# Two transformer layers on one core: the opening of layer 0, with its Q and K traffic spread over three queues and side work moved later

## The chip, the core and the metric

The kernel runs on one core of a Trainium2 chip. A core has five engines, each with its own instruction queue that it works through in order: TensorE (PE in the profile, its weight loads PEld), VectorE (DVE), ScalarE (ACT), GpSimd (POOL) and SyncE (SP), which here only issues DMA transfers. ScalarE and GpSimd can issue DMA transfers too, from the same in-order queue as their arithmetic. Engines wait for each other by semaphores. Sixteen DMA engines carry all transfers of the core.

The metric is the time of one execution in microseconds on the device. Lower is better.

## The reference

Two layers work on x of 2 x 1024 x 256. Each adds an attention and a feed-forward part to x, both computed from the same layernorm of x. Only layer 0 is touched by the change:

```python
xn = layernorm(x)
# attention: 32 query heads and 8 key/value heads of 8 columns, causal
q = rope((xn @ Wq + bq).heads(32));  k = rope((xn @ Wk + bk).heads(8));  v = (xn @ Wv + bv).heads(8)
scores = where(kpos > qpos, -inf, q @ repeat(k, 4).T / sqrt(8))
attn = softmax(scores) @ repeat(v, 4) @ Wo + bo
# feed-forward in e4m3: every operand of a product is rounded to e4m3 first
ffn = (gelu(xn8 @ w_gating8[0]) * (xn8 @ w_gating8[1]))8 @ w_linear8
x = x + attn + ffn
```

Layer 1 is an attention with 16 heads over 512-token sequences and a gated feed-forward part with ternary weights.

## The kernel before

**Tiles.** The 2048 tokens are 16 tiles of 128 (`xs`), four to a chunk; a batch `b` has two chunks `c` and eight tiles `i`. `layernorm` (L153) is a generator: statistics of four tiles to a step, then the inverse root (`rsqrt`, L139: VectorE, a square root on ScalarE with its own activation table, VectorE), then per chunk four normalised rows `xn`, and a step of eight transposes `lnt` on TensorE and two copies into `xnT` on ScalarE.

**Q and K.** Q and K are split into three bf16 parts each, and a score is a sum of products of parts over 64 + 35 rows. `project` (L713) multiplies `xnT` with the weights into two PSUM banks, applies bias and rope with two `scalar_tensor_tensor` on VectorE (L729) and adds them; `split` (L701) makes the three parts by turns of ScalarE casts (L704, L707) and subtractions (L706, L708), on VectorE for batch 0's chunk 0, on GpSimd otherwise. The parts are rearranged by a round trip through DRAM: written to a scratch (`kscr`, `qscr`) and loaded back in the order that the score products need. For K, `prepare_k` (L736) writes once and loads 18 pieces of 8 rows x 4 x 512. For Q, `prepare_q` (L756) makes one half `e` of the heads for a whole chunk and writes each of its four tiles by itself; `load_q` (L766) loads one tile: for each half two pieces of 24 rows, one of 16 and one of 8, each row 4 KB. `qlast` are four buffers for the last 35 rows, cleared at the start.

**Softmax.** The maximum of every row is needed before the exponentials. `max_unit` (L835) multiplies queries with keys for a few heads and VectorE reduces the product (L858); `take_max` splits a tile's maxima into three parts, and `turn_max` (L879) transposes them on TensorE, copies them to `mt` on ScalarE, writes them to DRAM (`mscr`) and loads them into three rows of `qlast`. Only then can `weigh` (L905, one unit of head group `u` and key tile `j`) multiply again, now with the maximum subtracted, and ScalarE takes the exponential (L920). `gather` accumulates p times v.

**The order.** TensorE's order in layer 0 is written by hand: a loop over slots (`one_slot`, L1108), one to a unit of weighing. In each slot the maxima of later tiles are advanced by a credit so that they run ahead of the weighing, one piece of the feed-forward work is emitted (`pieces`, `pieces_left`), and delayed steps fall due (`after`). When the maxima reach tile number n of the order, the list `extra[n]` is set free, one entry with each following unit. In `extra` stand, for tile 0, chunk 1's layernorm and its K; for tile 1, chunk 1's Q and V; for tile 2, the layernorm of batch 1 (`second`); for 4, 6 and 7, batch 1's Q, K and V. The other engines are ordered by a scheduler that takes instructions as they become ready. `tc.issue_after(ins)` holds a block's instructions behind `ins` on that instruction's own engine; `behind()` does so with `mark`, the last normalised row or the last subtraction of a split on VectorE.

**The feed-forward weights.** `weights0` (L203) loads six pieces of 512 KB and rounds each to e4m3 in five steps on VectorE (`e4m3`, L182: L190, L193, L195, L198, L200). Before Q and K are prepared, the first load is issued from SP and three steps of the first conversion are set on VectorE, behind `mark`.

**The start.** SP issues, in this order: four tiles of x, rope of chunk 0, the three weights, five small constants, four more tiles of x, the first feed-forward piece; then K's write and 18 loads, Q's eight writes and the loads of tiles 0 to 3, rope of chunk 1 and `wo` among them, and the other tiles of x.

## Time and profile before

| | |
|---|---|
| median of three runs | 1212.17 us (1210.58 to 1214.08) |
| the profiled execution's own time | 1211.61 us |
| its span, first to last instruction | 1209.9 us |
| PE busy | 1026.2 us, 85%, 7228 matmuls |
| DVE busy | 741.5 us, 61%, 1416 instructions |
| ACT busy | 571.7 us, 47% |
| POOL busy | 348.4 us, 29% |
| mean granted TensorE clock | 0.897 |
| first reduction of a maximum (L858) | 48.21 us |
| first complete weighing (L910) | 104.47 us |

The span is the time from the first to the last instruction of the profiled execution; the own time of that execution is 1.7 us more. Lines of the timeline give start and duration in microseconds, the engine, the source line, the operation with the tile that it writes and those that it reads, how many were merged, and in brackets how long the engine had been idle and what ended that. SPq is SP's queue of DMA issues: its durations are those of issuing, not of the transfer. Lines of waits give the waiting instruction, what it waited for, the total, how often, and the longest. Lines of windows give the stretch, its length, busy time of PE, PEld, DVE, ACT and POOL with instruction counts, the granted TensorE clock as a share of full speed, the mean busy share of the 16 DMA engines, and GB/s. Layer 0 takes up about the first 800 us.

### The profile page before, as it was taken

How to read it: one execution, taken by the hardware profiler on the slowest of the kernel's cores; microseconds unless marked ns; L12 is line 12 of the kernel's file. 1: busy time of each engine (PE TensorE's matmuls, PEld its weight loads, DVE VectorE, ACT ScalarE, POOL GpSimd, SP SyncE). 2: the span in 40 equal slices, each digit the busy share in tenths (PEclk: the TensorE clock that was granted, in tenths of full speed). 3: DMA queues.
4: the chain of work that ended last, by engine and by line, in shares of the span. 5: the costliest groups of instructions: out<-in, count | busy, mean ns of one | idle time of the engine just before them, and what ended most of it. 6: DMA issues, size and time to landing. Idle time of an engine off the chain costs nothing.

```text
span 1209.9 us, 18918 instructions
## 1 busy us (share of the span) xinstructions
PE 1026.2 (85%) x7228; PEld 490.2 (41%) x7228; DVE 741.5 (61%) x1416; ACT 571.7 (47%) x990; POOL 348.4 (29%) x400
## 2 busy tenths in 40 slices
PE   5464888896888989897989998988999999998884
PEld 2232332232232222232323333344676676675673
DVE  6677988995877998789895889162223323322220
ACT  1113353661645757576766776731414414424421
POOL 2023233314144021612125337553313213212100
PEclk8676796996898989898999999998999999998885
DMA  6631001103001010101010110047211421411202
GB/s 194 158 91 37 22 15 38 27 2 90 1 20 33 2 26 18 35 1 24 4 27 2 25 27 5 3 49 114 41 28 46 75 41 45 80 36 29 45 11 53
DMA packets 79011, 48.99 MB, mean 40 GB/s; under 512 B 31720, under 2 KB 73704, under 8 KB 78920
## 3 DMA queue, kind: packets, MB, share of 16 engines
q1 hardware_dynamic: 75960, 43.58, 16.9%
q0 software_dynamic: 2960, 4.20, 1.6%
q8 instruction: 57, 0.93, 0.3%
q14 instruction: 34, 0.28, 0.1%
HBM read 33.59 MB, written 15.73 MB: 41 GB/s over the span
## 4 chain that ended last, share of the span: by engine, by line
PE 55%; DVE 26%; ACT 5%; issue 4%; POOL 4%; DMA 4%; SPq 1%; ACTq 0%; POOLq 0%; DVEq 0%
DVE mx L858 14%; PE f1gu L609 9%; PE acc L940 8%; PE s L910 7%; PE f1o L640 5%; PE m L846 4%; PE sk L519 3%; PE sq L484 3%; PE gu L283 3%; ACT p L527 2%; PE m L823 2%; PE acc L534 1%; PE ao L585 1%; PE pqk L435 1%; ACT p L920 1%
## 5 line engine op out<-in xcount | busy, mean ns | idle before, releaser
L858 DVE TENSOR_REDUCE mx<-m 128x1 f32<-128x512 f32 (+3 forms) x608 | 373.1, 654 | 101.5 <-PE m L846 63.1
L920 ACT ACTIVATE p<-s 128x512 f32<-128x512 f32 x576 | 307.1, 604 | 146.3 <-PE s L910 144.8
L940 PE MATMUL acc<-p,v 128*9 128x512 f32 x1152 | 173.7, 626 | 0.6 <-ACT o L949 0.2
L846 PE MATMUL m<-k,qmain 64*128 64x512 bf16 (+3 forms) x384 | 96.6, 376 | 49.2 <-DVE mx L858 33.0
L924 POOL TENSOR_SCALAR_AFFINE_SELECT p<-p 128x512 f32<-128x512 f32 x128 | 84.6, 685 | 170.1 <-ACT p L920 169.9
L609 PE MATMUL f1gu<-xnT,wgu 128*128 128x512 f32 x256 | 118.5, 607 | 0.0
L846 PE MATMUL m<-kmain,qmain 64*128 64x512 bf16 (+3 forms) x384 | 82.8, 336 | 22.9 <-DVE mx L858 20.7
L846 PEld LDWEIGHTS <-qmain 64*128 64x128 bf16 x768 | 50.4, 101 | 88.4 <-issue 62.9
L621 POOL TENSOR_TENSOR sq<-h 128x512 f32<-128x512 f32 x28 | 29.2, 1041 | 190.1 <-DVE h L617 190.1
L617 DVE TENSOR_TENSOR h<-f1gu,h 128x512 f32<-128x512 f32 x32 | 22.1, 692 | 99.7 <-PE f1gu L609 96.4
L910 PE MATMUL s<-qlast,k 35*128 35x512 bf16 x288 | 66.5, 411 | 14.6 <-DMA qlast<-mscr 14.6
L910 PE MATMUL s<-qmain,k 64*128 64x512 bf16 x288 | 68.6, 412 | 11.8 <-ACT ob L251 6.2
L823 PEld LDWEIGHTS <-ident_h 64*128 64x128 bf16 x832 | 44.9, 97 | 82.5 <-issue 60.3
L823 PE MATMUL m<-mask_q,ident_h 64*128 64x128 bf16 (+3 forms) x832 | 75.3, 222 | 2.5 <-DVE mx L858 2.2
L910 PE MATMUL s<-qmain,kmain 64*128 64x512 bf16 x288 | 64.0, 391 | 6.0 <-ACT p L920 3.2
L910 PEld LDWEIGHTS <-k 64*128 64x128 bf16 (+1 forms) x576 | 21.2, 97 | 115.7 <-issue 108.2
L609 PEld LDWEIGHTS f1gu<-xnT,wgu 128*128 128x128 f32 x256 | 48.0, 197 | 49.2 <-issue 49.1
L492 DVE TENSOR_REDUCE m<-sq 128x16 f32<-128x2048 f32 x16 | 36.7, 2292 | 45.3 <-PE sq L484 43.8
L910 PE MATMUL s<-qlast,klast 35*128 35x512 bf16 x288 | 61.3, 387 | 0.0
L640 PE MATMUL f1o<-k,h 128*128 128x256 f32 x256 | 60.4, 393 | 0.0
L640 PEld LDWEIGHTS f1o<-k,h 128*128 128x128 f32 x256 | 50.1, 197 | 8.7 <-issue 1.1
L983 POOL TENSOR_TENSOR x<-x,aos 128x256 f32<-128x256 f32 x16 | 13.1, 817 | 140.1 <-ACT aos L982 140.0
(265 smaller groups left out, 1572.4 us busy)
## 6 DMA issues: line engine op xcount, KB each, us to landing
qmain<-qscr SPq DMA_DIRECT2D x64, 96.0 KB
qkv<-all SPq DMA_DIRECT2D x16, 384.0 KB
qscr<-ptq SPq DMA_DIRECT2D x32, 96.0 KB
x<-in_x SPq DMA_DIRECT2D x16, 128.0 KB
qmain<-qscr SPq DMA_DIRECT2D x32, 64.0 KB
qs<-qkv SPq DMA_DIRECT2D x16, 128.0 KB
ks<-qkv SPq DMA_DIRECT2D x16, 128.0 KB
vs<-qkv SPq DMA_DIRECT2D x16, 128.0 KB
```

Of the source, the lines that this page charges most:

```text
L283: nc.tensor.matmul(ps, wg[:, u, k, hc * P : (hc + 1) * P], xq[:, k, :], start=(k == 0), stop=(k == 1))
L484: nc.tensor.matmul(ps[:, s, r, :], columns(q, slice(S * s, S * s + HD + 8), 4 * b + r), columns(k, slice(S * s, S * s + HD + 8), 4 * b + r ...
L492: nc.vector.tensor_reduce(m, ps, AX.X, ALU.max, negate=True)
L609: nc.tensor.matmul(ps[g], wgu[:, k, g * HID + hc * P : g * HID + (hc + 1) * P], xnT[n][:, k, :], start=(k == 0), stop=(k == 1),)
L640: nc.tensor.matmul(po, hs[hc // 2][:, hc % 2, i * P : (i + 1) * P], wp[:, hc, :], start=(hc == 0), stop=(hc == NHC - 1),)
L823: nc.tensor.matmul(out[e][:, :, lo:], ident_h[rows, t, :], rhs.to_broadcast([HALF, out[e].shape[1], P - lo]), start=start and t == 0, stop ...
L846: nc.tensor.matmul(sc[e][:, s * width : (s + 1) * width], qst[b, i][0][rows, p, :], kst[b][0][rows, p // 4, lo : lo + width], start=not fo ...
L858: reduced = nc.vector.tensor_reduce(mx[b, i][:, part, e, pairs[0] : pairs[0] + n], sc[e][:, : n * width].rearrange("p (s k) -> p s k", s=n ...
L910: nc.tensor.matmul(sc[e], kst[b][n][rows, u, j * P : (j + 1) * P], qst[b, i][n][rows, 4 * u : 4 * u + 4, :], start=n == 0, stop=n == 1,)
L920: nc.scalar.activation(p, sc[e], AF.Exp, scale=scale)
L924: nc.gpsimd.affine_select(out=by_head, in_=by_head, compare_op=ALU.is_ge, fill=0.0, base=0, pattern=[[0, 4], [1, P]], channel_multiplier=-1,)
L940: nc.tensor.matmul(acc[32 * s : 32 * s + HD0 + 1, :], vst[b][:, j, 4 * G + s, :], ps[s], start=(j == 0), stop=(j == i),)
```

## The change

The change rearranges the opening of layer 0. What is computed stays the same.

- Four of the small constants are issued first of all, from ScalarE's queue; `bo` from SP after the second four tiles of x.
- The feed-forward weights' first load is issued from GpSimd like the others. `next(conversions)`, which only issues that load, stands after K's preparation, and the three conversion steps before it are gone: they become pieces of the slot loop (`pieces_left` 156 + 18 instead of 156 + 15).
- K's write is issued from GpSimd except for batch 0's chunk 0, and there three of the 18 loads go to GpSimd.
- Q's four writes per half become one of 12 pieces of 128 columns, from GpSimd, or from ScalarE for batch 0's chunk 0. The scratch keeps the four tiles of a chunk together, so a tile's load now reads blocks of 8 rows that lie apart; tile 0's loads are issued from ScalarE.
- Chunk 1's Q, K and V move from the start of the maxima of tiles 0 and 1 to those of tile 2, K after Q; the layernorm of batch 1 from tile 2 to tile 3, with its VectorE instructions held behind the last reduction.
- `mt` has two buffers.

```diff
@@ -106,11 +106,10 @@
         nc.sync.dma_start(out=rope[:, :, c * 512 : (c + 1) * 512], in_=a["rope0"][:, :, c * 512 : (c + 1) * 512])
 
     def load_small():
-        nc.sync.dma_start(out=bq, in_=a["bq"])
-        nc.sync.dma_start(out=bk, in_=a["bk"])
-        nc.sync.dma_start(out=inv_freq, in_=a["inv_freq"][None, :].to_broadcast([P, 8]))
-        nc.sync.dma_start(out=bv_bc, in_=a["bv"][None, :].to_broadcast([P, 64]))
-        nc.sync.dma_start(out=bo_bc, in_=a["bo"][None, :].to_broadcast([P, D]))
+        nc.scalar.dma_start(out=bk, in_=a["bk"])
+        nc.scalar.dma_start(out=bq, in_=a["bq"])
+        nc.scalar.dma_start(out=bv_bc, in_=a["bv"][None, :].to_broadcast([P, 64]))
+        nc.scalar.dma_start(out=inv_freq, in_=a["inv_freq"][None, :].to_broadcast([P, 8]))
 
     def load_weights(pool, names):
         w = []
@@ -211,8 +210,7 @@
         def load(n):
             st = stage[n % 4]
             if n < 4:
-
-                (nc.sync if n < 1 else nc.gpsimd).dma_start(out=st, in_=a["w_gating"][n // 2, n % 2 * P : n % 2 * P + P, :])
+                nc.gpsimd.dma_start(out=st, in_=a["w_gating"][n // 2, n % 2 * P : n % 2 * P + P, :])
             else:
                 nc.gpsimd.dma_start(
                     out=st.rearrange("p (c d) -> p c d", d=D),
@@ -744,24 +742,25 @@
                     engine.memset(kst[b][1].bitcast(F32), TWO_ONES)
                 parts = project(wk, 0, P, bk, b, c, f"k{b}{c}")
                 scr = dram.tile([3, HD0, 16, 512], BF, tag="kscr", name=f"kscr{b}{c}")
-                nc.sync.dma_start(out=scr.rearrange("a d n t -> (d n) a t"), in_=parts)
+                (nc.gpsimd if b or c else nc.sync).dma_start(out=scr.rearrange("a d n t -> (d n) a t"), in_=parts)
                 for e in range(2):
                     for n, (_, ka) in enumerate(MAIN + [LAST]):
                         lo = HALF * e + HD0 * (n % 8)
-                        nc.sync.dma_start(
+
+                        queue = nc.sync if b or c or e == 0 or n % 3 else nc.gpsimd
+                        queue.dma_start(
                             out=kst[b][n // 8][lo : lo + HD0, :, c * 512 : (c + 1) * 512],
                             in_=scr[ka, :, 4 * e : 4 * e + 4, :],
                         )
 
             def prepare_q(b, c, e):
                 parts = project(wq, e * P, 2 * P, bq[:, :, e], b, c, f"q{b}{c}{e}")
-                for i in range(4):
-                    scr = scratch[b, 4 * c + i, e] = dram.tile(
-                        [3, P, P], BF, tag=f"qscr{i}{e}", name=f"qscr{b}{4 * c + i}{e}"
-                    )
-                    nc.sync.dma_start(
-                        out=scr.rearrange("a p t -> p a t"), in_=parts[:, :, i * P : (i + 1) * P]
-                    )
+                scr = scratch[b, c, e] = dram.tile([3, 4, P, P], BF, tag=f"qscr{e}", name=f"qscr{b}{c}{e}")
+
+                (nc.gpsimd if b or c else nc.scalar).dma_start(
+                    out=scr.rearrange("a i p t -> p (a i) t"),
+                    in_=parts.rearrange("p a (i t) -> p (a i) t", i=4),
+                )
 
             def load_q(b, i):
 
@@ -770,12 +769,12 @@
                     qlast[len(qst) % len(qlast)],
                 ]
                 for e in range(2):
-                    parts = scratch[b, i, e].rearrange("a (d h) t -> (a d) h t", d=HD0)
-                    for n, lo, rows in ((0, 0, 24), (0, 24, 24), (0, 48, 16), (1, 0, 8)):
-                        start = 16 if n else 0
-                        last_load[0] = nc.sync.dma_start(
-                            out=qst[b, i][n][HALF * e + lo : HALF * e + lo + rows],
-                            in_=parts[start : start + rows],
+                    parts = scratch[b, i // 4, e][:, i % 4].rearrange("a (d h) t -> a d (h t)", d=HD0)
+                    for n, row, lo, hi in ((0, 0, 0, 3), (0, 24, 0, 3), (0, 48, 0, 2), (1, 0, 2, 3)):
+                        row += HALF * e
+                        last_load[0] = (nc.sync if b or i else nc.scalar).dma_start(
+                            out=qst[b, i][n][row : row + HD0 * (hi - lo)].rearrange("p h t -> p (h t)"),
+                            in_=parts[lo:hi],
                         )
 
             def prepare_v(b, c):
@@ -879,7 +878,7 @@
             def turn_max(b, i, parts):
                 ps = ps_t.tile([P, P], BF, tag="t", name=f"mt{b}{i}")
                 nc.tensor.transpose(ps[: 3 * NH0], parts.rearrange("p a h -> p (a h)"), ident_bf)
-                mt = pool.tile([3 * NH0, P], BF, tag="mt", name=f"mts{b}{i}", bufs=1)
+                mt = pool.tile([3 * NH0, P], BF, tag="mt", name=f"mts{b}{i}", bufs=2)
                 nc.scalar.copy(mt, ps[: 3 * NH0])
                 scr = dram.tile([3 * NH0, P], BF, tag="mscr", name=f"mscr{b}{i}")
                 nc.sync.dma_start(out=scr, in_=mt)
@@ -996,13 +995,12 @@
             spare = [x.rearrange("p u t -> p (u t)").bitcast(F32) for x in spare]
             conversions = weights0(pool, [x[:, n * 1024 : (n + 1) * 1024] for x in spare for n in range(2)])
             rest_of(layernorm(0, [0], pool, ps_t, "t"))
-            weights = next(conversions)
             with behind():
                 for t in qlast:
                     nc.vector.memset(t, 0.0)
-                for _ in range(3):
-                    next(conversions)
             prepare_k(0, 0)
+            with behind():
+                weights = next(conversions)
             for e in range(2):
                 prepare_q(0, 0, e)
             load_q(0, 0)
@@ -1033,14 +1031,18 @@
                 with behind():
                     next(first)
 
+            def next_second():
+                with tc.issue_after(reduced.ins):
+                    next(second, None)
+
             def pause():
                 pass
 
             extra = {
-                0: [lambda: next(first)] + [next_first] * 2 + [lambda: next(first), lambda: prepare_k(0, 1)],
-                1: [lambda e=e: prepare_q(0, 1, e) for e in range(2)] + [lambda: prepare_v(0, 1)],
-                2: [lambda: next(second)] * 4 + [pause] * 2 + [lambda: next(second), lambda: next(second)]
-                + [pause, lambda: rest_of(second)],
+                0: [lambda: next(first)] + [next_first] * 2 + [lambda: next(first)],
+                2: [lambda e=e: prepare_q(0, 1, e) for e in range(2)]
+                + [lambda: prepare_k(0, 1), lambda: prepare_v(0, 1)],
+                3: [next_second] * 4 + [pause] * 2 + [next_second] * 2 + [pause] + [next_second] * 2,
                 4: [lambda e=e: prepare_q(1, 1, e) for e in range(2)],
                 6: [lambda: rest_of(conversions)]
                 + [lambda c=c: prepare_k(1, c) for c in range(2)]
@@ -1087,7 +1089,7 @@
             credit = share = 0.0
             cost_left = sum(cost for _, cost, _ in maxima)
             pairs_left = sum(4 * (i + 1) for _, i in order)
-            pieces_left = 156 + 15
+            pieces_left = 156 + 18
             done_at = {}
 
             def advance():
@@ -1147,10 +1149,11 @@
                 next_late()
 
 
+    load_small()
     load_rope(0)
     w0 = load_weights(zp, ("wk0", "wq0", "wv0"))
-    load_small()
     load_x(4, 8)
+    nc.sync.dma_start(out=bo_bc, in_=a["bo"][None, :].to_broadcast([P, D]))
     qlast = [zp.tile([P, NH0 // 2, P], BF, tag=f"qlast{n}", name=f"qlast{n}") for n in range(4)]
     tables = []
     attention0(w0, qlast, tables)
```

## The prediction

> **What bounds the kernel now.** I read the shares of busy time first, then the times of the opening from the timeline, then who waited for whom between 60 and 110 us, and last the busy time by stage. The whole run has TensorE busy for 85% of its span and VectorE for 61%. That average hides the place of this change, so the first two lines below are TensorE and VectorE in 40 slices of 30 us.
>
> ```profile
> PE   5464888896888989897989998988999999998884
> DVE  6677988995877998789895889162223323322220
> ...
> 20.52 0.69 DVE L190 TENSOR_SCALAR few<-spare_main 128x1024 int32<-128x1024 int32 x1 [6.79 <-DMA spare_main<-in_w_gating]
> 21.13 0.75 DVE L729 SCALAR_TENSOR_TENSOR k00y<-k00p,bk,rope 128x512 f32<-128x512 f32 x1
> 28.23 0.38 SPq L747 DMA_DIRECT2D kscr<-ptk  x1
> 30.78 6.53 SPq L751 DMA_DIRECT2D k<-kscr  x18
> 36.70 0.69 DVE L708 TENSOR_TENSOR ptq<-restq,ptq 128x512 bf16<-128x512 f32 x1 [0.68 <-ACT ptq L707]
> 37.40 4.29 SPq L762 DMA_DIRECT2D qscr<-ptq  x8
> 41.74 1.28 SPq L776 DMA_DIRECT2D qmain<-qscr  x3
> 47.66 0.58 PE L846 MATMUL m<-k,qmain 64*128 64x128 bf16 x7 [1.62 <-DMA qlast<-qscr]
> 48.21 1.29 DVE L858 TENSOR_REDUCE mx<-m 128x4 f32<-128x512 f32 x2 [6.13 <-PE m L846]
> ```
>
> TensorE is at half or less for 120 us. VectorE sits for 6.79 us before L190, an FFN weight conversion whose data has not come, and K's first step (L729), ready since 16.4 us, stands behind it. Only after the splits come 18 K loads, 8 Q writes and the Q loads, all one after another on SP. The first maximum is taken at 48.21 us. The next stage has its own wait:
>
> ```profile
> POOL restq L706 <- ACT ptq L704: 20.9, 2, 20.1
> ACT rs_sln L145 <- DVE rs_vln L144: 17.4, 1, 17.4
> ...
> PE s L910 <- DMA qlast<-mscr: 14.6, 1, 14.6
> ```
>
> ScalarE waits 17.4 us with the square root of the second layernorm at the head of its queue. Behind it stands chunk 1's Q split, behind that GpSimd's, behind that SP's write of Q, and behind that the maxima of tile 0; so TensorE's first weighing (L910) waits 14.6 us, until 104.47. The last view is busy time by stage:
>
> ```profile
> core 0: us, PE busy (x) PEld busy (x) DVE busy (x) ACT busy (x) POOL busy (x), PEclk, DMA share, GB/s
> 0.00:48.20 48.20, 20.83 (x61) 10.39 (x62) 31.11 (x89) 8.06 (x13) 8.20 (x25) 0.79 0.60 171
> 48.20:106.60 58.40, 32.59 (x209) 18.15 (x208) 39.59 (x84) 9.05 (x15) 12.46 (x12) 0.65 0.36 96
> 106.60:151.50 44.90, 36.46 (x268) 16.44 (x267) 42.18 (x76) 17.95 (x35) 13.49 (x17) 0.77 0.12 28
> 151.50:166.00 14.50, 13.28 (x112) 5.36 (x110) 11.14 (x18) 11.02 (x22) 2.45 (x4) 1.00 0.01 1
> ...
> 291.50:297.50 6.00, 4.93 (x18) 2.46 (x18) 3.94 (x11) 0.00 (x0) 0.16 (x1) 0.50 0.33 94
> 142.00:145.00 3.00, 1.32 (x9) 0.59 (x10) 3.00 (x5) 0.00 (x0) 1.38 (x1) 0.86 0.72 172
> ```
>
> Before 106.6 us (the second unit of weighing, u1) VectorE is idle for 17.1 + 18.8 us: latency rules. From there to 151.5 it is busy for 42.2 of 44.9 us: VectorE rules. Then TensorE does, with 13.3 of 14.5. So what is gained in the first stage must still pass one in which VectorE has no room.
>
> **The change, part by part.** Durations are of this execution, whose own time is 1211.61 us; the median of three is 1212.17.
>
> *Conversion moved off the first split; small loads to ScalarE's queue.* K's first L729 can start when the four memsets of qlast end (13.7 us), the second when its matmuls end (16.4), so it ends at 17.2 instead of 23.1. The rest of K's split took 5.1 us from there with three conversion steps between; with layernorm statistics in their place I take 4.7: K is split at 21.9, not 28.2. From there to the end of Q's split stays 9.2 us: 31.1 instead of 37.4. Four issues of about 0.5 us stand ahead of ScalarE's table load (1.28), which then ends near 4.2, before its first input at 6.0: nothing. The weights' issues are still at the head of GpSimd's queue in the changed order (one before mask_q's selects, three behind its iota): only the arithmetic moves. Chunk 1's rope and wo (768 KB) now start before K's write; at the 289 GB/s of 2 to 16 us all early bytes are in by about 22, so the bounds are 0 and 1 us and I take 0, the row of K's write being near that end.
>
> *K and Q by three queues.* K's write starts at 21.9 and its 15 SP loads (0.363 each) about 2.5 later; three go to GpSimd. ScalarE issues Q's two writes (0.53 each) behind its own casts, the second at 31.1; with 2.1 us to land (K's write took that) its four loads go out by 35.3. Before, the last Q load took 3.1 us to land: 38.4. ScalarE's issues hold what is queued behind them: the sine's table load, the sine, the table load and square root of chunk 1's layernorm (1.28 + 0.31 + 1.28 + 0.20), then five VectorE steps (1.2). Both ways end near 40. First maximum at 40 instead of 48.2.
>
> *The Q loads' new shape.* A load of 24 rows was one run of 24; its source is now 3 blocks of 8, and that of 16 rows 2 blocks of 8. The trace has no such load. Its bounds: nothing, if the spread over DMA engines stays; or as many engines as blocks. That a load's outermost loop sets its engines is what the last two lines above suggest: with only K loads moving (8 rows) the DMA share is 0.33 and never over half, with Q loads it is 0.72. A tile's 144 rows of 4 KB took 39 engine-us, 0.27 each; at the 25 GB/s per engine of 10 to 12 us a row takes 0.16. With 50 rows on the busiest engine a tile takes 8 to 13.6 us there instead of some 4. Tile 0's halves then land at 39.7 to 45, the following tiles' every 8 to 13.6 us. Chunk 0's maxima want tile 1 at about 50 and tile 2 at 66: at 0.2 a row they wait 1.5 us in all, which I take, being between the two rows; at 0.27 they wait 9.
>
> The Trainium skill (DMA: Bandwidth & Descriptors, Why a DMA increments its semaphore by 16 and not by 1) says that the engines used are the largest number up to 16 that divides the outermost size on both sides, and that they are the lowest-numbered. By it 24 rows went to 12 engines and now go to 3, and 16 rows to 2 instead of 16: the upper bound's case, against the change; without it the sum below would be 1.5 us better.
>
> *Projections and second layernorm later.* From 40 on VectorE has to do: tile 0's 8 reductions (5.2), four normalisations (1.4), one conversion and three steps of another (6.4), the splitting of maxima (0.75), tile 1's 16 reductions (10.3): 24, with 2 of waits 66. Before, chunk 1's K and Q came between tiles 0 and 1, and 55.2 to 75.5 saw six reductions. They are not saved: Q now stands between tile 2's first two units, four half projections of 2.5 us in a row with the reductions between, 11 us to tile 1's turn of maxima, 3.3 more through ScalarE, two small DMAs (1.6, 1.8) and TensorE: 80.3. K's projection (4.9) and V's (2.0) stand before the second unit of weighing: 9.5 more, 90, and 91.5 with the Q loads. That is 15 us before today's 106.6.
>
> *What of it lasts.* Three things are still owed at that point: the second layernorm's statistics, root and first four rows (8.5 of VectorE), and 2.9 of conversion, less one unit's reductions (1.0) done early. By tile 3's ninth unit (151.5 before) 4.3 of conversion is still put off, so VectorE has 5.5 us more to do in a stage where it has 2.7 free, and there it must wait for a square root with its table load (about 1.5). I take 51 us instead of 44.9. The next stage has 3.1 more VectorE work in 3.4 us of room: 15 instead of 14.5. So 91.5 + 51 + 15 = 157.5 against 166.0: 8.5 us remain.
>
> *Behind that.* Of the writes moved from SP to GpSimd six are batch 1's. GpSimd's rows for an issue run from 0.55 to 0.79; K's and Q's stretches (270 to 285, 346 to 363) have GpSimd on the chain. 6 x 0.7 = 4.2, half on the path: 2 (bounds 0 and 5, for larger patterns). SP's Q write no longer blocks the maxima's write (9.77 us on SP at 353, when TensorE had other work): 0 to 2 gained, taken at 0. About three FFN pieces stay behind, some 4 us spread over 550: 1. The second buffer for mt and the later bo cost nothing: neither is waited for. Sum: 8.5 - 2 - 1 = 5.5, so 1211.6 - 5.5 = **1206.1 us**.
>
> **Rivals.** (1) *All kept:* the shift at 91.5 or better stays because later stages are TensorE's. For it: from 125 to 750 us VectorE is idle for about 100 us in all. Against: 106.6 to 151.5. Gain 11 to 15: 1198. (2) *Debt paid in full:* VectorE absorbs nothing and a few more us go where GpSimd issues. For it: 42.2 of 44.9. Gain 0 to 3: 1210. (3) *Slower:* the Q loads of the first four tiles on few engines. At 0.27 a row W00's second unit comes at 99, and the stage after takes the rest: about 1213. From 0.3 a row on it decides: at 0.4, 20 us per tile, tile 3 lands at 110, SP's maxima writes stand behind it and the first weighing is at 115, 10 later: 1220. For it: nothing shows one engine alone with 25 rows queued; against it: a longer queue per engine ran faster (10 to 12 us), not slower. (4) *It does not do what it says:* weights are not loaded behind anything; if their transfers were what held K, K's first step would still wait. Against: rope had landed by 7.5, when SP passed its reuse. Gain then 0 to 3, with (2).
>
> **How the numbers follow.** Mine 0.45; all kept 0.14; debt in full and (4) 0.18; slower 0.23. Faster takes nearly all of mine and the first: 0.57; 0.3% (3.6 us, about what a measurement of this kernel can tell) holds the rest of mine and most of the third: 0.20; slower 0.23. The range goes from all kept at 14 (1198) to the slower case at 0.33 a row (1217). My own case alone would be 1202 to 1209.
>
> **What would show it.** K's write near 22 us and the first maximum at 40 (38 to 46); tile 1's units without projections between; no wait of ScalarE for a root of 10 us; first weighing near 82; tile 3's last reduction at 158. I am wrong if TensorE waits for Q loads of tiles 1 to 3, if VectorE is not the busiest from 90 to 140, or if GpSimd's issues take several us each.

## The result and the profile after

The changed kernel takes 1217.45 us (median of 20 runs, 1210.88 to 1224.27), the kernel before 1212.1 us in the runs beside it (1206.78 to 1214.08). The ratio is 1.0046, with a 95% interval of 1.003 to 1.0062: slower by about half a per cent, on the other side of my forecast of 1206.1 and just outside its range of 1198 to 1217. The changed kernel also scatters nearly twice as much. Its profiled execution is the fastest of the 20 (own time 1210.88, span 1209.1), so it shows where things stand but hides part of the loss; a second profile follows below.

The page's lines of TensorE and VectorE in 40 slices, of the changed kernel:

```profile
PE   5377888896889888887989988988999999998884
...
DVE  6668988887878898797986889162223323322220
```

TensorE's poor stretch at the start is shorter by a slice. Past the middle of layer 0 (slices 14 to 24) it now has an 8 in five slices that had a 9. Both halves of the story are already there.

The opening, from the timeline:

```profile
17.13 0.75 DVE L727 SCALAR_TENSOR_TENSOR k00y<-k00p,bk,rope 128x512 f32<-128x512 f32 x1 [1.14 <-PE k00p L716]
...
23.48 0.38 SPq L745 DMA_DIRECT2D kscr<-ptk  x1
...
26.06 16.31 SPq L751 DMA_DIRECT2D k<-kscr  x15
...
28.02 0.40 ACTq L760 DMA_DIRECT2D qscr<-ptq  x1
...
31.43 1.31 ACTq L775 DMA_DIRECT2D qmain<-qscr  x1
...
33.20 1.70 ACTq L775 DMA_DIRECT2D qmain<-qscr  x2
...
37.39 3.28 ACTq L775 DMA_DIRECT2D qmain<-qscr  x3
...
45.98 0.58 PE L845 MATMUL m<-k,qmain 64*128 64x128 bf16 x7 [5.64 <-DMA k<-kscr]
...
46.52 1.29 DVE L857 TENSOR_REDUCE mx<-m 128x4 f32<-128x512 f32 x2 [1.21 <-PE m L845]
```

The conversion no longer stands before K, and K's write goes out 4.8 us earlier (23.48 against 28.23). But SP now spends 16.31 us on 15 K loads, where 18 took 6.53, and the first maximum comes at 46.52, only 1.7 us earlier. The merged line of the K loads hides gaps between them: the sixth goes out at 28.07, the seventh at 31.37. That first gap lies behind GpSimd's three K loads (26.32 to 28.00) and ScalarE's first write of Q (28.02) and ahead of ScalarE's first load.

Who waited between 40 and 110 us:

```profile
PE m L845 <- DMA k<-kscr: 17.7, 2, 12.1
...
PEld L845 <- DMA qlast<-qscr: 5.8, 1, 5.8
...
PE s L909 <- DMA qlast<-mscr: 2.1, 1, 2.1
```

The first weighing's wait for the maxima has shrunk from 14.6 to 2.1 us: that part of the change did what it says. The two lines above it are those of tile 0; no later tile of Q is waited for.

Busy time by stage, the bounds being the first maximum, the second unit of weighing, the fourth finished output and the splitting of tile 3's maxima, which begins 1 us after their last reduction (columns as in the prediction):

```profile
0.00:46.50 46.50, 17.36 (x61) 9.45 (x62) 26.29 (x80) 9.35 (x14) 9.67 (x28) 0.83 0.56 177
46.50:91.60 45.10, 33.44 (x223) 19.43 (x222) 34.33 (x65) 6.34 (x11) 12.23 (x13) 0.72 0.32 98
91.60:140.60 49.00, 37.04 (x244) 13.96 (x241) 43.44 (x96) 20.25 (x37) 18.16 (x20) 0.79 0.16 51
140.60:157.40 16.80, 14.98 (x120) 6.09 (x117) 16.73 (x27) 10.77 (x22) 3.34 (x5) 1.00 0.00 1
```

VectorE fills the last of these wholly, 16.73 of 16.80 us: the debt that the prediction spoke of is being paid here. Even so tile 3's last reduction ends at 156.4 us instead of 166.2.

**Where the lead goes.** ScalarE copies the output of a finished head group out of PSUM 32 times in layer 0 (`o<-acc`, L949 before, L948 after). These starts are milestones that both kernels share:

| output | before, us | changed, us | lead |
|---|---|---|---|
| 1st | 111.4 | 101.7 | 9.7 |
| 5th | 164.6 | 153.9 | 10.7 |
| 13th | 405.2 | 393.7 | 11.5 |
| 17th | 539.0 | 528.7 | 10.3 |
| 20th | 627.9 | 625.8 | 2.1 |
| 27th | 761.2 | 760.9 | 0.3 |
| 32nd | 792.7 | 792.4 | 0.3 |

At the 13th output VectorE has done 615 instructions, against 616 before: its debt is paid, and a lead of 11.5 us is there. It is lost afterwards. What differs there is which feed-forward piece stands beside which unit: three conversion pieces came into the queue in front, so every later piece comes a few units later in TensorE's order. The stretch from the 13th to the 27th output, as one window each, of the kernel before and of the changed one:

```profile
405.19:761.21 356.02, 316.86 (x2514) 106.88 (x2512) 301.84 (x594) 240.96 (x459) 117.83 (x146) 0.96 0.07 17
```

```profile
393.69:760.88 367.19, 319.99 (x2526) 109.75 (x2524) 308.20 (x594) 243.89 (x461) 120.49 (x146) 0.95 0.06 16
```

VectorE runs 594 instructions in both, but is busy 6.4 us longer with them, and the stretch is 11.2 us longer. TensorE has a dozen weight loads and matmuls more in it (2524 weight loads for 2512), which stood ahead of the 13th output before; at 0.13 us, the mean of a matmul there, that is some 1.5 us by estimate.

### The profile page after: what moved, and what is told of

It is laid out like the page before. It is cut to its first block, busy times and chain, and to the rows that moved or that the text cites. A ratio compares the mean times of both kernels' runs of the same rounds, so it can differ in the third digit from the quotient of the medians.

```text
span 1209.1 us, 18893 instructions
## 1 busy us (share of the span) xinstructions
PE 1025.0 (85%) x7228; PEld 489.1 (40%) x7228; DVE 749.2 (62%) x1416; ACT 575.1 (48%) x992; POOL 363.1 (30%) x413
## 4 chain that ended last, share of the span: by engine, by line
PE 51%; DVE 29%; POOL 6%; ACT 5%; DMA 5%; issue 3%; SPq 0%; ACTq 0%; POOLq 0%; DVEq 0%
DVE mx L857 15%; PE f1gu L607 8%; PE acc L939 7%; PE s L909 6%; PE f1o L638 5%; PE m L845 3%; PE sk L517 3%; PE sq L482 3%; PE gu L281 2%; ACT p L525 2%; PE acc L532 2%; PE m L822 1%; PE ao L583 1%; DMA qs<-in_same 1%; PE ot L954 1%
## 5 line engine op out<-in xcount | busy, mean ns | idle before, releaser
L919 ACT ACTIVATE p<-s 128x512 f32<-128x512 f32 x576 | 308.2, 602 | 151.8 <-PE s L909 149.6
L939 PE MATMUL acc<-p,v 128*9 128x512 f32 x1152 | 178.7, 633 | 4.0 <-POOL p L923 2.8
L845 PE MATMUL m<-k,qmain 64*128 64x512 bf16 (+3 forms) x384 | 99.5, 370 | 57.8 <-DVE mx L857 38.1
L923 POOL TENSOR_SCALAR_AFFINE_SELECT p<-p 128x512 f32<-128x512 f32 x128 | 87.1, 702 | 160.6 <-ACT p L919 160.3
L822 PEld LDWEIGHTS <-ident_h 64*128 64x128 bf16 x832 | 45.1, 98 | 92.0 <-issue 71.4
L490 DVE TENSOR_REDUCE m<-sq 128x16 f32<-128x2048 f32 x16 | 36.7, 2292 | 43.1 <-PE sq L482 41.5
```

Source lines behind the costliest of these rows:

```text
L490: nc.vector.tensor_reduce(m, ps, AX.X, ALU.max, negate=True)
L822: nc.tensor.matmul(out[e][:, :, lo:], ident_h[rows, t, :], rhs.to_broadcast([HALF, out[e].shape[1], P - lo]), start=start and t == 0, stop ...
L845: nc.tensor.matmul(sc[e][:, s * width : (s + 1) * width], qst[b, i][0][rows, p, :], kst[b][0][rows, p // 4, lo : lo + width], start=not fo ...
L919: nc.scalar.activation(p, sc[e], AF.Exp, scale=scale)
L923: nc.gpsimd.affine_select(out=by_head, in_=by_head, compare_op=ALU.is_ge, fill=0.0, base=0, pattern=[[0, 4], [1, P]], channel_multiplier=-1,)
L939: nc.tensor.matmul(acc[32 * s : 32 * s + HD0 + 1, :], vst[b][:, j, 4 * G + s, :], ps[s], start=(j == 0), stop=(j == i),)
```

## The experiments

The theory that formed from the table (called A on record) says that the shifted pieces cost the lead; its rivals were GpSimd's long DMA issues (C), and that any lead would run off later, wherever the pieces stand (D).

| kernel | median, us | ratio to before, 95% | 5th output | 13th | 27th | 13th to 27th |
|---|---|---|---|---|---|---|
| before (profile) | 1212.1 | | 164.6 | 405.2 | 761.2 | 356.0 |
| changed (first profile) | 1217.45 | 1.003 to 1.0062 | 153.9 | 393.7 | 760.9 | 367.2 |
| changed, again | 1216.83 | 1.0025 to 1.0059 | 153.9 | 393.8 | 766.3 | 372.5 |
| order alone | 1210.77 | 0.9963 to 0.9995 | 148.0 | 387.6 | 760.1 | 372.5 |
| queues alone | 1204.94 | 0.992 to 0.9962 | 164.2 | 402.6 | 757.4 | 354.8 |
| changed, 180 pieces | 1215.72 | 0.9992 to 1.0039 | 156.9 | 403.1 | 767.7 | 364.6 |
| order, pieces as before | 1201.8 | 0.9912 to 0.994 | 154.0 | 394.7 | 750.8 | 356.1 |
| changed, pieces as before | 1205.25 | 0.9935 to 0.9968 | 160.1 | 398.6 | 753.6 | 355.0 |
| changed, constants from SP | 1218.41 | 1.0053 to 1.0093 | 153.1 | 396.8 | 766.9 | 370.1 |
| changed, chunk 0 from SP | 1219.54 | 1.0055 to 1.0096 | 158.8 | 401.1 | 772.9 | 371.8 |
| the same, Q by tiles | 1213.45 | 0.999 to 1.0035 | 150.1 | 390.0 | 760.8 | 370.8 |
| before, 3 empty pieces | 1221.12 | 1.0055 to 1.0109 | 158.5 | 397.6 | 768.6 | 371.0 |
| order, steps behind Q | 1198.76 | 0.9868 to 0.9904 | 154.2 | 391.2 | 746.8 | 355.6 |
| the same, late writes from GpSimd | 1196.82 | 0.985 to 0.989 | 152.3 | 390.7 | 745.6 | 354.9 |

Each ratio is to runs of the kernel before on the same chip, whose medians lie between 1211.2 and 1213.0. The outputs are those of one profiled execution each. The last column falls into two groups. Where TensorE's order past tile 3 is that of before it is 354.8 to 356.1; where the pieces stand elsewhere it is 364.6 to 372.5. In all of the latter the offset of the pieces and their spacing (`pieces_left`) were changed together; which of the two matters was not tried.

**The changed kernel again.** No edit.

> The changed kernel unaltered, for a second profiled execution: the first was the fastest of 20. In that one the opening's lead of 10 us (tile 3's last weighing units 10.7 us earlier) lasted until 540 us and was gone by 727, in stretches where TensorE has the half clock. Theory A (the lead is given back to half-clock stretches after VectorE lulls): a typical execution, at 1215 to 1220, has the same lead of 9 to 11 us at 166 us and loses 14 to 18 by 750, with the granted clock at 1.0 for less of the time than in the first profile; layer 1 takes the 412 us of before. Theory B (the opening itself varies, by DMA landing): the lead at 166 us is only 2 to 5 us, and the loss after 540 is the 10 us of the first profile.

Own time 1214.3 in the profile. The lead is 10.7 at the 5th output and 11.4 at the 13th, as in the first; at the 27th it is 5.1 us behind (layer 1 then takes 2.3 us less than before, 414.8 for 417.2). So the opening is the same to 0.1 us in both executions, and the scatter lies in the later stretch: 372.5 here, 367.2 in the first. From 400 to 540 us the granted clock is 0.89, against 0.96 in the first. B, that the opening itself varies, falls.

**Each half alone.** First the order alone: against the kernel before, the hunks of the change that move the conversions and fill `extra`, with their piece count, the first feed-forward load from GpSimd and the second buffer of `mt`.

```diff
-            weights = next(conversions)
             with behind():
                 for t in qlast:
                     nc.vector.memset(t, 0.0)
-                for _ in range(3):
-                    next(conversions)
             prepare_k(0, 0)
+            with behind():
+                weights = next(conversions)
...
+                2: [lambda e=e: prepare_q(0, 1, e) for e in range(2)]
+                + [lambda: prepare_k(0, 1), lambda: prepare_v(0, 1)],
+                3: [next_second] * 4 + [pause] * 2 + [next_second] * 2 + [pause] + [next_second] * 2,
...
-            pieces_left = 156 + 15
+            pieces_left = 156 + 18
```

Then the queues alone: against the kernel before, the hunks of `load_small`, `prepare_k`, `prepare_q`, `load_q` and the start.

```diff
+                (nc.gpsimd if b or c else nc.sync).dma_start(out=scr.rearrange("a d n t -> (d n) a t"), in_=parts)
...
+                        queue = nc.sync if b or c or e == 0 or n % 3 else nc.gpsimd
...
+                (nc.gpsimd if b or c else nc.scalar).dma_start(
+                    out=scr.rearrange("a i p t -> p (a i) t"),
...
+                        last_load[0] = (nc.sync if b or i else nc.scalar).dma_start(
```

> The kernel before with the order of the change alone: conversions behind K's split and three more pieces in the slots, chunk 1's Q, K, V at tile 2, second layernorm at tile 3; all queues and the layout of Q's scratch as before. Theory A (order: where the pieces and reductions fall after 500 us makes TensorE wait for VectorE and drop to the half clock): the whole loss shows, 1213 to 1220. Theory C (GpSimd's long issues: six writes of Q at 1.06 us each and three of K at 0.79): this kernel has none of them and keeps most of the opening's lead, 1202 to 1208.

> The kernel before with the queues of the change alone: small constants from ScalarE, K's and Q's writes from GpSimd and ScalarE, three K loads from GpSimd, Q's scratch by chunk and its loads in blocks of 8 rows; conversions, projections and second layernorm as before. Theory A: the order from 166 us on is that of before, so what little the queues gain or lose stays: 1208 to 1213. Theory C: slower, 1214 to 1220, with the loss at 270 to 290 and 346 to 366 us where GpSimd issues the writes on the chain.

Neither number was foreseen well. The order alone has a lead of 16.6 us at the 5th output, six more than the changed kernel, and loses it to 1.1 by the 27th: 372.5 us for the stretch. The queues alone have no lead at the 5th output (0.4) and are 2.6 ahead at the 13th, and they keep it: 354.8. C falls twice: the kernel without GpSimd's issues has the loss, the kernel with them does not. In its profile the kernel with the queues alone is 3.8 us ahead at the last output: 3.3 are gained from the 9th to the 10th output (46.4 for 49.7) and 2.2 from the 11th to the 12th (44.4 for 46.6), the stretches of batch 1's K and Q, and 3.7 are lost from the 5th to the 6th. Its median gains about twice as much as its profile; where the rest lies stays open.

The first maximum of the order alone, and of the queues alone:

```profile
42.44 1.29 DVE L857 TENSOR_REDUCE mx<-m 128x4 f32<-128x512 f32 x2 [6.11 <-PE m L845]
```

```profile
52.65 1.29 DVE L858 TENSOR_REDUCE mx<-m 128x4 f32<-128x512 f32 x2 [1.85 <-PE m L846]
```

So in the opening the queues with the loads' new shape cost time: 4.4 us against before (48.21), and 4.1 us in the change (46.52) against the order alone.

**Another offset.**

```diff
-            pieces_left = 156 + 18
+            pieces_left = 156 + 24
```

> The changed kernel with the feed-forward pieces spread as if there were 180 instead of 174: each falls a little earlier and the last are done before the weighing ends. Nothing else changes. Theory A: the place of the pieces decides the lulls after 500 us, so the time moves by more than its uncertainty, to 1206 to 1213 if the three pieces that the conversions put behind were the reason, and upward if it is only a matter of luck. Theory C: unchanged within 2 us of the changed kernel, 1216 to 1219.

Theory A missed this one: 1215.72 is within 2 us of the changed kernel, as C expected. The stretch is shorter than in the change (364.6), but the lead is gone by the 8th output already (0.1 us behind). Two other offsets than that of before were tried, then, and both are worse in that stretch; whether a third is better was not tried.

**The pieces put back in step.** The three conversion steps are taken out of the slots and set among tile 1's maxima; from tile 3's tenth unit on TensorE's order is that of before.

```diff
+            def next_conversion():
+                with tc.issue_after(reduced.ins):
+                    next(pieces)
...
+                1: [next_conversion] * 3,
...
-            pieces_left = 156 + 18
+            pieces_left = 156 + 15
```

> The order of the change with the queues of before, and the three conversion steps put into tile 1's maxima instead of the feed-forward slots (pieces 156 + 15): from tile 3's tenth unit of maxima on TensorE's order is that of before, piece for piece. Theory A (the shifted pieces): from the 13th to the 27th head group's output it takes the 355 us of before instead of the 372 of the order alone, so most of the 17 us of lead stays: 1196 to 1202. Theory D (whatever lead there is at 400 us goes into half-clock stretches and waits, wherever the pieces lie): 372 again and 1208 to 1213.

> The changed kernel with the three conversion steps put into tile 1's maxima and 156 + 15 pieces, so that TensorE's order from tile 3's tenth unit of maxima on is that of before. Theory A: 355 us instead of 367 to 372 between the 13th and the 27th output, a lead of 9 to 11 kept to the end: 1200 to 1205. Theory D: 1213 to 1218, as the changed kernel.

With these few lines the changed kernel goes from 1217 to 1205.25 and the order alone from 1210.77 to 1201.8. In the latter the lead is 10.4 to 10.6 us at every output from the 5th to the 32nd. In the profile of the former it is 4.5 at the 5th, 6.6 at the 13th and 7.6 at the 27th. D falls: a lead is kept where the pieces are in step.

**The other way round.** The opening of before, no lead sought, and three pieces that do nothing ahead of the others.

```diff
-            pieces = itertools.chain(conversions, ffn0(pool, ps_t, weights, add_done))
+            pieces = itertools.chain([None] * 3, conversions, ffn0(pool, ps_t, weights, add_done))
...
-            pieces_left = 156 + 15
+            pieces_left = 156 + 18
```

> The kernel before, opening untouched, with three empty pieces ahead of the feed-forward ones (156 + 18), so that from tile 3's tenth unit of maxima on TensorE's order is that of the changed kernel; no work is added, moved or removed in the opening. Theory A (the shifted pieces are the whole loss): 364 to 372 us between the 13th and the 27th head group's output instead of 356, and a time of 1220 to 1228. Theory D (the loss is the lead going elsewhere; without a lead there is none to lose): 356 and 1210 to 1214.

The stretch from the 13th to the 27th output of this kernel:

```profile
397.60:768.60 371.00, 326.41 (x2517) 110.50 (x2524) 308.98 (x594) 243.92 (x462) 120.13 (x146) 0.92 0.07 16
```

15 us longer than before with the same 594 instructions on VectorE and all of the opening's order untouched. From the 5th output to the 32nd TensorE's order in this trace is that of the changed kernel. The 15 us are not all loss, though: with no lead sought, this kernel is 6.1 us ahead at the 5th output, where VectorE has three instructions less behind it (261 for 264), and 7.6 at the 13th. In the end it is 7.4 us behind before at the 32nd output, and 8.8 by the medians (1221.12 for 1212.35). The shift of the pieces is a cause by itself, and a lead at the 13th output can in part be the shift's own.

**What the shift does there.** The same point in both kernels, in windows of 2 us: four normalised rows of layer 1's layernorm on VectorE beside a ternary weight on GpSimd. The kernel before:

```profile
555.00:557.00 2.00, 2.00 (x12) 0.58 (x10) 2.00 (x4) 0.47 (x1) 1.85 (x2) 0.50 0.01 1
557.00:559.00 2.00, 0.71 (x5) 0.13 (x2) 2.00 (x3) 1.68 (x4) 1.92 (x2) 0.96 0.06 12
559.00:561.00 2.00, 0.49 (x1) 0.00 (x0) 2.00 (x5) 0.00 (x0) 1.18 (x2) 0.89 0.00 0
561.00:563.00 2.00, 2.00 (x11) 0.26 (x12) 1.97 (x5) 0.00 (x0) 0.00 (x0) 0.50 0.59 66
563.00:565.00 2.00, 2.00 (x14) 1.01 (x10) 0.81 (x3) 1.04 (x2) 0.00 (x0) 0.76 0.00 0
```

The changed kernel:

```profile
545.00:547.00 2.00, 2.00 (x16) 0.41 (x10) 2.00 (x4) 0.13 (x2) 1.84 (x3) 0.69 0.08 16
547.00:549.00 2.00, 0.71 (x7) 0.10 (x2) 2.00 (x4) 2.00 (x4) 1.92 (x2) 1.00 0.03 12
549.00:551.00 2.00, 0.03 (x1) 0.00 (x0) 2.00 (x4) 0.00 (x0) 1.65 (x2) 0.67 0.00 0
551.00:553.00 2.00, 2.00 (x9) 0.12 (x8) 2.00 (x4) 0.00 (x0) 0.00 (x0) 0.50 0.61 65
553.00:555.00 2.00, 2.00 (x12) 0.59 (x9) 0.51 (x2) 0.57 (x2) 0.00 (x0) 0.50 0.01 1
```

VectorE is full in both until the fourth row, and TensorE runs dry waiting for its reductions. The clock falls to half after that, for one unit of the trace's clock record before and for two in the change; at half clock TensorE is the slow one and VectorE runs dry in turn (0.51 of 2 us). From the 17th to the 18th output, with four such units against two, the changed kernel takes 43.1 us instead of 37.9. In the clock records every stretch of half clock between 100 and 1100 us is a multiple of 3.41 us. From the 13th to the 27th output there are 9 such units before, 11 in the first profile of the changed kernel, 17 in its second and with empty pieces, 16 with the order alone, and 8 in the two best kernels below. By estimate a unit costs TensorE at most half of it, 1.7 us: the 8 more units make up to 13.6 of the 15 to 16.5 us, the 2 more of the first profile 3.4 of its 11.2. The Trainium skill (TensorE: Matmul & The Clock Gate, What's actually happening) gives a free-running window of some 3.4 us and half the clock after an idle one; the multiples of 3.41 us agree.

Another part may be VectorE's own time: 301.8 to 303.8 us for its instructions in the stretch where the pieces are in step, 308.2 to 310.0 where they are shifted by three. How much of that delays TensorE is not shown. Nor do the two parts explain every case: with 180 pieces VectorE takes 303.3 us and there are 11 units, and the stretch is 8.6 us longer than before all the same. The group of one instruction of the feed-forward pieces, in the kernel before, then in the changed one, then with empty pieces:

```profile
L198 DVE TENSOR_TENSOR act<-fs,fe 128x1024 bf16<-128x1024 bf16 x16 | 11.8, 735 | 0.2
```

```profile
L197 DVE TENSOR_TENSOR act<-fs,fe 128x1024 bf16<-128x1024 bf16 x16 | 14.0, 872 | 0.3
```

```profile
L198 DVE TENSOR_TENSOR act<-fs,fe 128x1024 bf16<-128x1024 bf16 x16 | 14.0, 873 | 0.3
```

One of the lengthened ones, with what GpSimd does at that time, from two answers of the changed kernel's timeline:

```profile
561.36 1.10 DVE L197 TENSOR_TENSOR act<-fs,fe 128x1024 bf16<-128x1024 bf16 x1
```

```profile
560.45 1.47 POOL L923 TENSOR_SCALAR_AFFINE_SELECT p<-p 128x512 f32<-128x512 f32 x2 [9.51 <-ACT p L919]
```

The same instruction took 0.69 us before (at 566.15), when GpSimd was idle. That the two engines meet more often when the pieces fall elsewhere is read from such pairs, and was not tested by a run of its own. The Trainium skill (SBUF — State Buffer, Who interferes with whom) says that a VectorE instruction with two inputs in SBUF and a GpSimd instruction that reads SBUF exclude each other, whoever issues second waiting; the pair agrees.

**The opening, one part at a time.** First the constants.

```diff
-        nc.scalar.dma_start(out=bk, in_=a["bk"])
-        nc.scalar.dma_start(out=bq, in_=a["bq"])
...
+        nc.sync.dma_start(out=bq, in_=a["bq"])
+        nc.sync.dma_start(out=bk, in_=a["bk"])
...
-    load_small()
     load_rope(0)
     w0 = load_weights(zp, ("wk0", "wq0", "wv0"))
+    load_small()
```

> The changed kernel with the five small constants issued from SP behind the weights, as before. If the constants at the head of ScalarE's queue are what made the first layernorm late, its square root stands at 6.0 us instead of 9.1 and the first maximum comes 2 to 3 us earlier (43.5 to 44.5 instead of 46.5); if it is the feed-forward weights' load, which now starts from GpSimd beside x, the root stays at 9. By theory A and by D alike the time is 1213 to 1218, since the pieces lie where the change puts them.

The square root stands at 5.95 instead of 9.06, so the constants at the head of ScalarE's queue do delay the first layernorm by 3.1 us. It is worth nothing, against the 2 to 3 us expected: K's first step then waits until 18.08, K's write goes out at 23.25 (23.48 in the change) and the first maximum comes at 46.22.

Then the queues of chunk 0:

```diff
-                        queue = nc.sync if b or c or e == 0 or n % 3 else nc.gpsimd
+                        queue = nc.sync
...
-                (nc.gpsimd if b or c else nc.scalar).dma_start(
+                (nc.gpsimd if b or c else nc.sync).dma_start(
...
-                        last_load[0] = (nc.sync if b or i else nc.scalar).dma_start(
+                        last_load[0] = nc.sync.dma_start(
```

> The changed kernel with chunk 0's K loads, Q writes and tile 0's Q loads all issued from SP, as before; later chunks from GpSimd as in the change. If the three queues hold each other up there (the 15 K loads of SP took 16.3 us of issuing, 6.5 for 18 before), SP's K loads take 6 to 7 us, and the first maximum comes at 42 to 44 instead of 46.5. If ScalarE's queue only saves issue time, it comes at 48 or later. The time by A and D: 1213 to 1218.

And in addition Q of chunk 0 written and loaded by tiles, as before:

```diff
+                if not (b or c):
+                    for i in range(4):
+                        scr = scratch[i, e] = dram.tile(
+                            [3, P, P], BF, tag=f"qscr{i}{e}", name=f"qscr{b}{4 * c + i}{e}"
+                        )
...
+                if b == 0 and i < 4:
...
+                        parts = scratch[i, e].rearrange("a (d h) t -> (a d) h t", d=HD0)
+                        for n, lo, rows in ((0, 0, 24), (0, 24, 24), (0, 48, 16), (1, 0, 8)):
```

> The kernel with chunk 0's traffic on SP alone, and now chunk 0's Q written and loaded tile by tile in runs of 24 and 16 rows as before; later chunks as in the change. Its companion with blocks of 8 rows took its first maximum at 48.3 us. If the blocks of 8 rows, which a few DMA engines carry, are what holds tile 0, the first maximum is at 43 to 45, against the eight more issues on SP (0.55 each); if not, it is at 50 or later. The time by theory A: 1212 to 1217, for the pieces lie where the change puts them.

The first maximum of the one and of the other:

```profile
48.33 1.29 DVE L857 TENSOR_REDUCE mx<-m 128x4 f32<-128x512 f32 x2 [11.45 <-PE m L845]
```

```profile
42.83 1.29 DVE L876 TENSOR_REDUCE mx<-m 128x4 f32<-128x512 f32 x2 [6.28 <-PE m L864]
```

With all of it on SP the 18 K loads take 6.16 us again, and yet the maximum comes 1.8 us later than in the change: with these blocks the other two queues are worth that much. Q by tiles then brings it to 42.83, although SP issues six more DMAs: the blocks of 8 rows cost tile 0 5.5 us. It is not that the loads start sooner: the first of Q is issued at 36.11, at 35.55 with the blocks. While the next tiles' Q loads run, the last two columns (share of the 16 DMA engines, GB/s) show why. Blocks of 8 rows, then runs of 24 and 16:

```profile
48.00:52.00 4.00, 2.99 (x32) 2.08 (x28) 3.06 (x5) 0.00 (x0) 0.00 (x0) 0.50 0.21 81
52.00:56.00 4.00, 3.34 (x23) 2.52 (x20) 3.97 (x7) 0.17 (x1) 0.00 (x0) 0.50 0.22 76
```

```profile
48.00:52.00 4.00, 3.40 (x28) 2.55 (x25) 3.88 (x9) 1.07 (x2) 0.74 (x1) 0.62 0.76 159
52.00:56.00 4.00, 2.73 (x37) 1.89 (x37) 3.97 (x7) 0.26 (x1) 0.05 (x1) 0.81 0.88 202
```

0.21 of 16 engines is a little over three. The Trainium skill's rule on the number of engines (DMA: Bandwidth & Descriptors, Why a DMA increments its semaphore by 16 and not by 1), weighed in the prediction, made it 3 for a load of 24 rows; here the run agrees with it.

**Versions that keep the lead.** Against the order alone, the three steps go on VectorE behind Q's split:

```diff
             for e in range(2):
                 prepare_q(0, 0, e)
+            with behind():
+                for _ in range(3):
+                    next(conversions)
             load_q(0, 0)
...
-            pieces_left = 156 + 18
+            pieces_left = 156 + 15
```

> The order of the change on the queues of before, with the three conversion steps on VectorE behind Q's split, where it waits some 10 us for K's and Q's loads, instead of in tile 1's maxima; pieces 156 + 15. Theory A: 355 to 357 us between the 13th and the 27th output and the order's full lead of 14 to 16 us: 1195 to 1199. If those 10 us are not free for them, the first maximum comes later than 42.5 and the time is that of the steps in tile 1's maxima, 1201 to 1203.

In the second version every chunk but batch 0's first is written as in the change, and its Q loaded so:

```diff
-                nc.sync.dma_start(out=scr.rearrange("a d n t -> (d n) a t"), in_=parts)
+                (nc.gpsimd if b or c else nc.sync).dma_start(out=scr.rearrange("a d n t -> (d n) a t"), in_=parts)
...
+                scr = scratch[b, c, e] = dram.tile([3, 4, P, P], BF, tag=f"qscr{e}", name=f"qscr{b}{c}{e}")
...
+                (nc.gpsimd if b or c else nc.sync).dma_start(
```

> The kernel with the three steps behind Q's split, with K and Q of the later chunks written from GpSimd, Q by one write to a half as in the change; chunk 0 and the constants as before. If the later writes gain what the queues alone gained (3 to 8 us), 1190 to 1195; if that gain was the opening's, 1195 to 1199; if GpSimd's long issues cost, over 1200.

1198.76 and 1196.82: both beat both kernels, the second by 1.3% against before (ratio 0.987, 0.985 to 0.989). The stretch is 355.6 and 354.9. The first maximum comes at 43.0 and 43.7, so VectorE's wait there has room for the steps. The second kernel is 2.1 us behind the first at the 6th output, where GpSimd writes batch 1's first Q, and level with it at the 13th. The 1.9 us between the medians are within the two intervals: that the late writes gain on top is not shown.

## Why the prediction was wrong

- **Conversion moved off the first split.** Direction right, 1.5 us too early: K's write at 23.48, forecast 22. The price of nothing for four issues on ScalarE was wrong (the root 3.1 us later), but the run with the constants back on SP shows that it decides nothing.
- **K and Q by three queues, and the loads' shape.** Forecast 40 for the first maximum, measured 46.52. The order alone, on the queues of before, has it at 42.44, so what was to bring the rest of the gain cost 4.1 us. The mis-sized term is the shape: I took 1.5 us for all of chunk 0 and the runs show 5.5 at tile 0 alone (measured with everything on SP), while the later tiles, for which I had meant the term, were never waited for. The mechanism, few engines for blocks of 8 rows, was right. What I missed besides is that SP's K loads would stretch from 6.5 to 16.3 us beside the other two queues. Which of the two does it was not separated, nor was the shape of before tried on three queues.
- **Projections and second layernorm later.** The time is right, by luck: the first weighing's second unit is issued up to 91.62 (forecast 91.5, before 106.6), but from the first maximum to there I had counted 51.5 us and it took 45.1, which happens to cancel the 6.5 us by which that maximum was late. The first complete weighing stands at 83.5 (forecast 80.3).
- **What of it lasts.** Right as far as tile 3: its last reduction ends at 156.4, forecast 157.5, and VectorE filled the stage as said. But part of this lead is work put off, which I counted as lasting but for 1 us: the empty pieces alone show 6.1 at the 5th output, and the changed kernel with its pieces in step has 4.5 there instead of 10.7.
- **Behind that.** This is the step that failed. "About three FFN pieces stay behind, some 4 us spread over 550: 1" priced the pieces as work that is done later. The same event costs 9 to 12 us by the medians: the pieces move against the units of maxima beside them. The changed kernel with its pieces in step is 12.2 us faster (1205.25), the order alone 9.0 (1201.8), and three empty pieces, which add no work at all, make the kernel before 8.8 slower. The other term there was 2 us for GpSimd's issues. An issue takes longer than the 0.7 I took (1.06 us for a write of Q, 0.80 for K), but with the queues alone, from the 5th output to the 13th, where all of batch 1's writes lie, 2.2 us are gained on balance.

In sum, by the profiles at the 13th output: the order brought 17.6 us, the queues with the loads' shape took back 6.1, and 11.5 were left, three more than I had counted on, some of them perhaps the shift's own (the empty pieces alone have 7.6 there). The stretch behind then took 11.2 in the first profile and 16.5 in the second, and the median lies beyond the second.

Of the rivals, the slower one gave the right time (1213 to 1220) by the wrong place: the Q loads did come from few engines, but the first weighing stood at 83.5 and its second unit at 91.6, not at 99 to 115. "All kept", with its 11 to 15 us, was nearest until 540 us (leads of 7 to 12 from the 5th output to the 17th). "Debt paid in full" comes near the first profile's time, but VectorE had absorbed the debt by the 13th output. That the change does not do what it says is excluded by K's earlier write. The prediction named what would come late next only as far as tile 3. It named nothing that the change shifts for the 600 us behind. One reading of the lines was loose: TensorE's third slice before is a 6, so it is not at half or less for all of the first 120 us.

## What to carry to other kernels

Where an order is written by hand and two streams share engines, adding or taking out a few entries at the front of one stream shifts all of it against the other. Here that was worth 9 to 12 us where the work of the entries was priced at 1, so price it as a change of the whole stage; the cheap test is to add empty entries to the kernel before. When a start-up gain has been shown to reach the middle of a run and not its end, compare shared milestones along the run, and look for the stretch in which the same instructions take longer. Here the lead could be kept with the streams held in step, and with the old opening of the queues: 1196.8 us instead of 1217.

## What the runs showed of the hardware

- The same 594 instructions of VectorE took 301.8 us in one interleaving and 308.2 and 309.0 in the shifted one; a single bf16 instruction of 1024 columns took 1.10 us while GpSimd worked and 0.69 while it was idle.
- The half clock of TensorE comes in units of 3.41 us in these traces. Two profiles of one kernel, equal to 0.1 us at every output until 394 us, had 11 and 17 such units in the stretch behind and the last output of layer 0 5.3 us apart.
- 15 loads on SP's queue took 16.3 us to issue, with ScalarE's and GpSimd's queues issuing at the same time, and 18 took 6.2 without.
- While Q's next tiles were loaded, the 16 DMA engines were busy to 0.21 and 0.22 with blocks of 8 rows, to 0.76 and 0.88 with runs of 24 and 16.
